# A graph attention layer on one core: the low parts of a dense group by two wide instructions, counts cleared on ScalarE, one register load per round of edge sums

## The chip, the cores and the metric

The kernel runs on one core of a Trainium2 chip. The metric is the device time of one execution in microseconds; the time before is the median of three runs. A core has five engines that work side by side, each through its own list of instructions in order: TensorE (PE, matrix products), VectorE (DVE, elementwise work and reductions), ScalarE (ACT), GpSimd (POOL, here gathers by indirect DMA) and SyncE (SP, here DMA issues). They wait for each other by semaphores. SBUF is the memory of 128 partitions that all engines work from, PSUM the accumulators that TensorE writes.

## The reference

The layer takes 12,500 nodes of 64 features and 400,000 edges of 64 features, the edges sorted by destination. Cut to what matters:

```python
h_src, h_dst = x[src], x[dst]
e = leaky_relu(concat([h_src, h_dst, efeats]) @ W_attn + b_attn)[:, 0]
m = concat([h_src, efeats]) @ W_ne
ex = exp(e - segment_max(e, dst)[dst])
alpha = ex / segment_sum(ex, dst)[dst]
z = segment_sum(alpha[:, None] * m, dst)
out = layernorm(x + relu(concat([x, z]) @ W_out))
```

Destinations are drawn as the square of a uniform number, so the first nodes have very many edges and the later ones few.

## The kernel before

**Groups and batches.** Edges go in groups of 512 (P = 128 partitions, T = 4 edges each): 782 groups. The first DG = 104 are the *dense* groups, whose 512 edges go to a few nodes at most (NODS: 2 to 6). The other 678 are *sparse* groups and go through the main loop in 44 batches of up to 16, each cut in *lots* of four groups. Per sparse lot, POOL gathers the source rows (L310), ScalarE and VectorE make the scores (L341 to L362), and TensorE multiplies the gathered rows by weighted one-hot columns (L763); VectorE adds the products into a ring of node sums (L780, in `add_in`).

**Dense groups without gathers.** A dense group doesn't gather. A source node's number is split in a *low* part (modulo 128) and a *high* part (0 to 97). The matrix `counts` [128, 98, 16] holds, for a low part (partition), a high part and one of 16 destination slots, the summed weights of the edges between them. `dense_counts(g)` makes it for one group as four matrix products, one for each of the T edges of a partition (L458): on the left `lows`, whose row for an edge has the edge's weight `kept` at its low part and zero elsewhere; on the right `highs`, a one-hot row over high part and slot that ScalarE makes (L450, L451). `lows` is made on VectorE by `tensor_scalar` (L453), one instruction for each t: compare `count_` (0 to 127, kept in PSUM) with the edge's low part, times its weight, 128x128. `dense_sum` adds the product to `counts` (L475, and L478 for a sixth node).

**Chunks.** 25 times, after 2 to 9 dense groups, a chunk is closed: `node_products` multiplies `counts` with all node rows, in 13 steps (L525); `node_pick` takes the wanted diagonal blocks out of the product on VectorE (L533, L536) and clears `counts` for the next chunk (L538, a memset of 128x1568, for all chunks but the last); `node_turn` (L544) and `node_sum` (L550) put the sums in place.

**Edge features.** The edge features of the dense groups are summed by `edge_products` (L510) and `edge_sum` (L518). `edge_sum` handles a round, the two or three groups of one batch rounded up to four or two adds: for each it loads the first node of the group from `dn` into a register (`node_of`) and adds at that place. There are 34 rounds of four adds and one of two.

**The order.** DVE, PE, ACT and SP run in the order in which the program is written (`manual_schedule`), POOL issues its gathers likewise. In each batch the lots' scores come first, and with them `node_products` and `edge_products` (first lot) and the counts of the batch's first dense group (second lot). Then comes the softmax, a chain in four phases over VectorE, ScalarE and TensorE (transposes L556 and L559, scans L664 to L699, `turned` at L563). Between its phases `dense_step(n)`, n = 0 to 3, is laid: at n = 0 `node_pick`, `edge_sum` and `dense_sum`, then products of the batch before (L763) and `node_turn`; at n = 1 `node_sum`; at n = 2 and n = 3 the counts of the second and third dense group; and at each n the source scores of the dense groups to come (`look_scores`, L436 to L442, with L411 on TensorE). The sum of the second group comes at n = 3; that of the third between the first weights of the batch's own lots (L749). So the order on VectorE at n = 3 is: L475 of the second group, L780, `lows` of the third group, the end of the softmax, L749 and L475 of the third.

**Buffers.** `lows` are tiles of 128x128 from a pool of LOWS = 6. `kept` and `low` are in SBUF.

Of the kernel before, what the change touches and what calls it, by code (L numbers as in the profile page):

```python
# [9 lines left out]
F32 = mybir.dt.float32  # L10
I32 = mybir.dt.int32
AF = mybir.ActivationFunctionType
OP = mybir.AluOpType
AX = mybir.AxisListType

P = 128
T = 4
# [8 lines left out]
S = 48  # L26
BG = 32
BIG = 6
LOWS = 6
SG = 4  # L30
BS = 16
DO = BS + 1
# [10 lines left out]
ND = 16  # L43
# [11 lines left out]
EngineType = mybir.EngineType  # L55


def sorted_path(ctx, tc, x, dst, idx, edge, w_ne, w_attn, b_attn, w_out, out, flag):
# [6 lines left out]
    nc = tc.nc  # L65
    N, D = x.shape
    E = edge.shape[0]
    NB = (N + P - 1) // P
# [6 lines left out]
    within = "a destination is a node"  # L75

    const = ctx.enter_context(tc.tile_pool(name="const", bufs=1))
# [32 lines left out]
    def nodes_of(g):  # L110
        return next(n for upto, n in NODS if g < upto)
# [4 lines left out]
    def round_of(g):  # L116
        return max(d for d in range(DB) if begins[d] <= g)

    def kept_at(g):
        d = round_of(g)  # L120
        return g - begins[d] + d % 2 * BD
# [3 lines left out]
    DN = DBL * P  # L125
# [47 lines left out]
    low, place = (const.tile([P, T, DG], F32, name=n) for n in ("low", "place"))  # L173
    high, slot_ = (const.tile([P, T, DG], BF16, name=n) for n in ("high", "slot_"))
    y_dense = const.tile([P, T, 2 * BD], F32, name="y_dense")
    kept = const.tile([P, T, 2 * BD], F32, name="kept")
# [4 lines left out]
    acce = const.tile([P, DN + NOD], F32, name="acce")  # L181
    nc.vector.memset(acce, 0.0)
    edge_both = const.tile([P, D], F32, name="edge_both")
    dn = const.tile([1, DG + 1], I32, name="dn")
    rel = const.tile([1, DG], I32, name="rel")
    counts = const.tile([P, NB, ND], F32, name="counts")
# [3 lines left out]
    nc.vector.tensor_reduce(node, ident.rearrange("p (h n) -> p n h", n=ND), axis=AX.X, op=OP.add)  # L190
    meet = const.tile([1, 2], I32, name="meet")
    of_next = const.tile([1, 4], F32, name="of_next")
    scrap_row = const.tile([1, 1], F32, name="scrap_row")

    loop = ExitStack()
# [5 lines left out]
    def cut(bank, *widths):  # L201
        at, out_ = 0, []
        for w in widths:
            out_.append(bank[:, at:at + w])
            at += w
        assert at <= 512
        return out_
# [19 lines left out]
    pens, sixth, count_ = cut(pps, 2 * P, P, P)  # L227
    sixth, w_dst = sixth[:, 0:NB], sixth[:, 0:D]
# [164 lines left out]
    def big():  # L393
        return work.tile([P, P, T], F32, name="big", bufs=BIG)
# [48 lines left out]

    def dense_counts(g):

        highs, lows = [], []
        wide = NB * min(FIT, nodes_of(g))
        for t in range(T):
            hi = big().rearrange("l p t -> l (p t)")[:, 0:wide]
            nc.scalar.activation(hi, places[:, 0:wide], AF.Square, bias=place[:, t, g:g + 1])  # L450
            nc.scalar.activation(hi, hi, AF.Relu, scale=-1.0, bias=1.0)  # L451
            lows.append(work.tile([P, P], F32, name="lows", bufs=LOWS))
            nc.vector.tensor_scalar(lows[t], count_, low[:, t, g:g + 1], kept[:, t, kept_at(g):kept_at(g) + 1],  # L453
                                    op0=OP.is_equal, op1=OP.mult)
            highs.append(hi)
        to = psum.tile([P, SG, P], F32, name="pg", bufs=4).rearrange("p a b -> p (a b)")[:, 0:wide]
        for t in range(T):
            nc.tensor.matmul(to, lows[t], highs[t], start=(t == 0), stop=(t == T - 1))  # L458
        if nodes_of(g) > FIT:
            hi = big().rearrange("l p t -> l (p t)")[:, 0:T * NB].rearrange("l (t h) -> l t h", t=T)  # L460
            for t in range(T):
                nc.scalar.activation(hi[:, t], places[:, wide:wide + NB], AF.Square, bias=place[:, t, g:g + 1])
            nc.scalar.activation(hi, hi, AF.Relu, scale=-1.0, bias=1.0)
            for t in range(T):
                nc.tensor.matmul(sixth, lows[t], hi[:, t], start=(t == 0), stop=(t == T - 1), skip_group_check=True)
        return g, to

    def dense_sum(g, to):
# [23 lines left out]
    def node_of(g):  # L492
        _, vs = nc.values_load_multi_w_load_instructions(
            dn[0:1, g:g + 1], engines=(EngineType.DVE,), min_val=0, max_val=DN - 1,
            skip_runtime_bounds_check_because=within)
        return vs[0]
# [15 lines left out]

    def edge_sum(g0, n, z):

        for c in range(n + n % 2):
            of = slice(c % 2 * D, (c % 2 + 1) * D)
            at = acce[of, ds(node_of(g0 + min(c, n - 1)), nodes_of(g0))]
            nc.vector.tensor_tensor(at, at, z[of, c, :], op=OP.add)  # L518

    def node_products(g0):  # L520
# [8 lines left out]
    def node_pick(g0, pairs):  # L529

        pr = feats.tile([P, SG, T, D], F32, name="pr", bufs=1)
        mine = pr[:, 0:2].rearrange("p g t f -> p (g t) f")
        nc.vector.tensor_tensor(mine, pairs.rearrange("p (h f) -> p h f", f=D),  # L533
                                own.unsqueeze(2).to_broadcast([P, HC, D]), op=OP.mult)
        sums_ = work.tile([P, D], F32, name="sums_", bufs=1)
        nc.vector.tensor_reduce(sums_, mine.rearrange("p h f -> p f h"), axis=AX.X, op=OP.add)  # L536
        if g0 + chunk_sizes[-1] < DG:
            nc.vector.memset(counts, 0.0)  # L538
        return g0, sums_

    def node_turn(g0, sums_, bank_):
# [277 lines left out]
    with before:  # L819
# [22 lines left out]
        with tc.manual_schedule(engines={EngineType.DVE, EngineType.Pool, EngineType.Activation, EngineType.PE, EngineType.SP}):  # L842
# [21 lines left out]
            for g0 in range(0, NG, 3 * P):  # L864
                n = min(3 * P, NG - g0)
# [5 lines left out]
            at = 0  # L871
# [32 lines left out]
    work = loop.enter_context(tc.tile_pool(name="work", bufs=2))  # L904
# [138 lines left out]
    with loop:  # L1043
# [55 lines left out]
        with tc.manual_schedule(engines={EngineType.PE, EngineType.DVE, EngineType.Activation, EngineType.SP}):  # L1099
# [11 lines left out]
            for k, G in enumerate(sizes):  # L1111
# [19 lines left out]
                for i, (g0, n) in enumerate(lots[k]):  # L1131
# [32 lines left out]
                    if k and i == 1 and batch_counts:  # L1164
                        open_counts.append(dense_counts(batch_counts[0]))
# [36 lines left out]
                def dense_step(n):  # L1202

                    nonlocal opened, summed, resolved_at, node_z
                    if n == 0 and opened:
                        opened = node_pick(*opened)
                    if n == 0 and summed:
                        edge_sum(*summed)
                        summed = None
# [23 lines left out]
                    if n > 1:  # L1233
                        for g in batch_counts[1:2] if n == 2 else batch_counts[2:]:
                            open_counts.append(dense_counts(g))

                fac, joint, carry, carry_d = drawn(softmax(k, about, carry, joined, dense_carry if joined is not None else None), dense_step)
                if fac_d is not None and k > fac_at[1]:
                    at = node_of(fac_at[0])
# [421 lines left out]
@with_exitstack  # L1661
def kernel(
    ctx: ExitStack,
    tc: tile.TileContext,
    x: bass.AP,
    dst: bass.AP,
    idx: bass.AP,
    edge: bass.AP,
    w_ne: bass.AP,
    w_attn: bass.AP,  # L1670
    b_attn: bass.AP,
    w_out: bass.AP,
    out: bass.AP,
):


    nc = tc.nc
    mark = ctx.enter_context(tc.tile_pool(name="mark", bufs=1))
    flag = mark.tile([1, 1], I32, name="flag")
    with ExitStack() as own:  # L1680
        sorted_path(own, tc, x, dst, idx, edge, w_ne, w_attn, b_attn, w_out, out, flag)
    odd = nc.values_load(flag[0:1, 0:1], min_val=0, max_val=1,
                         skip_runtime_bounds_check_because="it is zero or one")
    with tc.If(odd > 0):
        with ExitStack() as own:
            general_path(own, tc, x, dst, idx, edge, w_ne, w_attn, b_attn, w_out, out)
# [51 lines left out]
```

## Time and profile before

| | |
|---|---|
| time, median of 3 runs | 4354.64 us (4350.4 to 4369.21) |
| profiled execution: time / span | 4348.44 us / 4346.6 us |
| granted TensorE clock, mean | 0.666 |
| busy PE / DVE / ACT / POOL | 53% / 49% / 27% / 59% of the span |
| gathers on POOL (L310) | 2648, 2499.3 us |
| product of lows and highs (L458) | 832 records (two for one product), 493.3 us |
| lows (L453) | 416, 141.5 us |
| clears of counts (L538) | 24, 32.8 us |
| edge sums (L518) | 138 |

The times come from one profiled execution. Busy time counts instructions that compute; register loads are not in it. In the rows of groups the columns are: line, engine, operation, tile written and tiles read, shape, count, busy time in us and mean of one in ns, and the idle time of the engine just before these instructions with what ended most of it. In the time line: start in us, duration, engine, line, operation, and in brackets how long the engine had been idle before and what it waited for ("issue": nothing that the profile shows). Records of matmuls show when TensorE takes them up; their results come later when older work is still in the array.

### The profile page before, as it was taken

The numbers are of one execution on the slowest core, as the hardware profiler recorded it, in microseconds if no ns is written. First come the engines' busy times: TensorE is split into PE (matmuls) and PEld (weight loads), VectorE is DVE, ScalarE is ACT, GpSimd is POOL, SyncE is SP. The second block draws the span as 40 slices with busy tenths as digits, with TensorE's granted clock in tenths as the row PEclk, the third lists the DMA queues.
The fourth block names the chain that finished last, engine by engine and source line by source line (L and its number), as shares of the span: only waits on it lengthen the run. The fifth ranks groups of instructions, "written<-read, shape, count | busy, mean of one in ns | idle before, by whom it ended". The sixth has DMA issues, their size and how long they took to land. (4 is left out here: it accounts for less than half of the span.)

```text
span 4346.6 us, 35943 instructions
## 1 busy us (share of the span) xinstructions
PE 2307.0 (53%) x9391; PEld 1840.8 (42%) x9391; DVE 2116.4 (49%) x5395; ACT 1165.9 (27%) x2586; POOL 2568.5 (59%) x2728
## 2 busy tenths in 40 slices
PE   0143344554555554655566665666566655565843
PEld 0143344444444444444444443444444434443543
DVE  4343344444444454554445554555555444453645
ACT  0111122222222232222223232332333223333312
POOL 6666666666556666566555655566555645555462
PEclk9999996555555555666566666666666656565655
DMA  9232223223232232322222222222223212222221
GB/s 116 57 64 52 53 55 73 56 56 69 45 67 57 55 63 58 68 54 57 56 58 63 60 55 56 56 57 58 56 57 74 57 31 47 50 49 43 58 46 26
DMA packets 497933, 248.42 MB, mean 57 GB/s; under 512 B 332351, under 2 KB 454286, under 8 KB 497718
## 3 DMA queue, kind: packets, MB, share of 16 engines
q1 hardware_dynamic: 407506, 155.16, 15.2%
q0 software_dynamic: 87008, 90.47, 13.6%
q8 instruction: 78, 1.28, 0.1%
q10 hardware_dynamic: 3204, 0.39, 0.1%
q14 instruction: 137, 1.12, 0.1%
HBM read 239.02 MB, written 6.77 MB: 57 GB/s over the span
## 5 line engine op out<-in xcount | busy, mean ns | idle before, releaser
L310 POOL DMA_INDIRECT zx<-table,srcs x2648 | 2499.3, 944 | 1683.0 <-issue 1239.6
L763 PE MATMUL pg<-w,zx 128*128 128x16 f32 (+9 forms) x5280 | 1042.6, 359 | 602.6 <-issue 548.0
L763 PEld LDWEIGHTS pg<-w,zx 128*128 128x128 f32 x5280 | 1061.4, 302 | 608.1 <-issue 549.0
L458 PE MATMUL pg<-big,lows 128*128 128x490 f32 (+3 forms) x832 | 493.3, 747 | 486.1 <-DVE lows L453 204.2
L458 PEld LDWEIGHTS pg<-big,lows 128*128 128x128 f32 x832 | 237.5, 300 | 669.7 <-issue 473.5
L525 PE MATMUL pg<-xall,counts 128*128 128x512 f32 (+1 forms) x650 | 326.7, 664 | 4.4 <-DVE var L1024 2.4
L344 DVE TENSOR_TENSOR pr<-ze,fixed 128x1024 f32<-128x1024 f32 (+3 forms) x176 | 207.5, 1179 | 224.4 <-issue 95.5
L411 PE MATMUL pg<-s_src,big 128*128 128x98 f32 x832 | 228.2, 433 | 164.1 <-issue 145.0
L556 PE MATMUL lines<-ident,bnd 128*1 128x128 f32 x176 | 52.8, 391 | 462.7 <-issue 342.1
L450 ACT ACTIVATE big<-places,place 128x490 f32<-128x490 int16 (+3 forms) x416 | 249.5, 600 | 155.3 <-remote 153.2
L411 PEld LDWEIGHTS pg<-s_src,big 128*128 128x128 f32 x832 | 209.0, 327 | 171.2 <-issue 170.6
L475 DVE TENSOR_TENSOR counts<-counts,pg 128x490 f32 (+3 forms) x104 | 58.1, 558 | 391.4 <-remote 311.4
L780 DVE TENSOR_TENSOR acc<-acc,pg 128x32 f32 (+9 forms) x678 | 125.8, 186 | 234.2 <-PE pg L763 106.0
L438 DVE TENSOR_TENSOR pr<-pr,pg 128x392 f32<-128x392 f32 x104 | 58.5, 562 | 354.9 <-remote 175.3
L346 DVE TENSOR_REDUCE fixed<-pr 128x16 f32<-128x1024 f32 (+3 forms) x176 | 209.2, 1188 | 32.2 <-issue 14.0
L451 ACT ACTIVATE big<-big 128x490 f32<-128x490 f32 (+3 forms) x416 | 217.2, 522 | 13.2
L556 PEld LDWEIGHTS lines<-ident,bnd 128*1 128x1 f32 x176 | 14.6, 98 | 485.9 <-issue 360.1
L525 PEld LDWEIGHTS pg<-xall,counts 128*128 128x128 f32 (+1 forms) x650 | 137.6, 219 | 188.8 <-issue 188.8
L563 ACT ACTIVATE line<-tops 1x256 f32<-1x256 f32 x44 | 29.0, 659 | 624.7 <-DVE tops L665 381.6
L342 ACT ACTIVATE zx<-ze 128x1024 f32<-128x1024 f32 (+3 forms) x176 | 181.0, 1028 | 8.3 <-issue 1.3
L341 ACT ACTIVATE fixed<-wrow 128x144 f32<-128x144 f32 (+9 forms) x176 | 46.0, 262 | 506.7 <-issue 321.7
L453 DVE TENSOR_SCALAR lows<-pps,low,kept 128x128 f32<-128x128 f32 x416 | 141.5, 403 | 0.0
(335 smaller groups left out, 2474.2 us busy)
## 6 DMA issues: line engine op xcount, KB each, us to landing
ze<-in_edge_dram SPq DMA_DIRECT2D x160, 512.0 KB
zx<-table,srcs POOLq DMA_INDIRECT x2648
low_of<-low_rows SPq DMA_DIRECT2D x104, 128.0 KB
ep<-in_edge_dram SPq DMA_DIRECT2D x104, 128.0 KB
ed<-in_edge_dram SPq DMA_DIRECT2D x34, 384.0 KB
table<-xall SPq DMA_DIRECT2D x7, 455.0 KB
ze<-in_edge_dram SPq DMA_DIRECT2D x8, 384.0 KB
out_dram<-yo SPq DMA_DIRECT2D x23, 128.0 KB
```

Of the source, the lines that this page charges most:

```text
L310: nc.gpsimd.indirect_dma_start(out=zx[0:r, g, t, 1:EW] if plain else zx[0:r, g, t, 0:EW], out_offset=None, in_=x[:, :] if plain else table ...
L342: nc.scalar.activation(zx[0:r, 0:n, :, EW:EW + D], ze[0:r, 0:n], AF.Copy)
L344: nc.vector.tensor_tensor(pr[0:r, 0:n], ze[0:r, 0:n], w_edge[0:r].unsqueeze(1).to_broadcast([r, n, T, D]), op=OP.mult)
L346: nc.vector.tensor_reduce(ysum[0:r, 0:n], pr[0:r, 0:n], axis=AX.X, op=OP.add)
L411: nc.tensor.matmul(found[:, t, :], hot[:, :, t], s_src, start=True, stop=True)
L450: nc.scalar.activation(hi, places[:, 0:wide], AF.Square, bias=place[:, t, g:g + 1])
L451: nc.scalar.activation(hi, hi, AF.Relu, scale=-1.0, bias=1.0)
L453: nc.vector.tensor_scalar(lows[t], count_, low[:, t, g:g + 1], kept[:, t, kept_at(g):kept_at(g) + 1], op0=OP.is_equal, op1=OP.mult)
L458: nc.tensor.matmul(to, lows[t], highs[t], start=(t == 0), stop=(t == T - 1))
L525: nc.tensor.matmul(pairs[0:m * ND, 0:m * D], counts[:, h0:h0 + m, :].rearrange("l h n -> l (h n)"), xall[:, h0:h0 + m, 1:EW], start=(h0 == ...
L763: nc.tensor.matmul(pg[:, g, :], zx[:, g, t, 1:EW + D], w[:, g, t, :], start=(t == 0), stop=(t == T - 1))
L780: nc.vector.tensor_tensor(ag, ag, pg[:, g, :], op=OP.add)
```

## The change

Three edits. First, `lows` of a group becomes one tile [128, 4, 128], made by two VectorE instructions of 128x512: a comparison of `count_` with the low parts, both broadcast, and then a product in place with the weights, broadcast; the tile comes from a pool of three. Their place in VectorE's order is where the four were. Second, `counts` is cleared by a ScalarE copy of a broadcast column of zeros instead of a VectorE memset; on ScalarE it stands between `bnd` of the softmax's first phase and L563. Third, `edge_sum` loads the registers of a round by one load instead of one for each add. The orders of PE, POOL and SP are the same as before.

```diff
-LOWS = 6
+LOWS = 3
...
+    zero_col = const.tile([P, 1], F32, name="zero_col")
+    nc.vector.memset(zero_col, 0.0)
...
     def dense_counts(g):

-        highs, lows = [], []
+        highs = []
+        lows = work.tile([P, T, P], F32, name="lows", bufs=LOWS)
+        nc.vector.tensor_tensor(lows, count_.unsqueeze(1).to_broadcast([P, T, P]),
+                                low[:, :, g:g + 1].to_broadcast([P, T, P]), op=OP.is_equal)
+        nc.vector.tensor_tensor(lows, lows, kept[:, :, kept_at(g):kept_at(g) + 1].to_broadcast([P, T, P]), op=OP.mult)
         wide = NB * min(FIT, nodes_of(g))
         for t in range(T):
             hi = big().rearrange("l p t -> l (p t)")[:, 0:wide]
             nc.scalar.activation(hi, places[:, 0:wide], AF.Square, bias=place[:, t, g:g + 1])
             nc.scalar.activation(hi, hi, AF.Relu, scale=-1.0, bias=1.0)
-            lows.append(work.tile([P, P], F32, name="lows", bufs=LOWS))
-            nc.vector.tensor_scalar(lows[t], count_, low[:, t, g:g + 1], kept[:, t, kept_at(g):kept_at(g) + 1],
-                                    op0=OP.is_equal, op1=OP.mult)
             highs.append(hi)
...
-            nc.tensor.matmul(to, lows[t], highs[t], start=(t == 0), stop=(t == T - 1))
+            nc.tensor.matmul(to, lows[:, t], highs[t], start=(t == 0), stop=(t == T - 1))
...
     def edge_sum(g0, n, z):

+        _, vs = nc.values_load_multi_w_load_instructions(
+            dn[0:1, g0:g0 + n], engines=(EngineType.DVE,), min_val=0, max_val=DN - 1,
+            skip_runtime_bounds_check_because=within)
         for c in range(n + n % 2):
             of = slice(c % 2 * D, (c % 2 + 1) * D)
-            at = acce[of, ds(node_of(g0 + min(c, n - 1)), nodes_of(g0))]
+            at = acce[of, ds(vs[min(c, n - 1)], nodes_of(g0))]
             nc.vector.tensor_tensor(at, at, z[of, c, :], op=OP.add)
...
         if g0 + chunk_sizes[-1] < DG:
-            nc.vector.memset(counts, 0.0)
+            nc.scalar.activation(counts.rearrange("p h n -> p (h n)"), zero_col.to_broadcast([P, NB * ND]), AF.Copy)
```

More of the change, by code (lines that the diff above doesn't have):

```diff
@@ L464, in dense_counts @@
             for t in range(T):
-                nc.tensor.matmul(sixth, lows[t], hi[:, t], start=(t == 0), stop=(t == T - 1), skip_group_check=True)
+                nc.tensor.matmul(sixth, lows[:, t], hi[:, t], start=(t == 0), stop=(t == T - 1), skip_group_check=True)
         return g, to
```

## The prediction

> **What bounds the kernel now.** I read the page first (busy times, then the costliest groups), then the list of waits, then the time line of single batches in the dense stage, which is where all three edits lie.
>
> ```profile
> PE 2307.0 (53%) x9391; PEld 1840.8 (42%) x9391; DVE 2116.4 (49%) x5395; ACT 1165.9 (27%) x2586; POOL 2568.5 (59%) x2728
> L310 POOL DMA_INDIRECT zx<-table,srcs x2648 | 2499.3, 944 | 1683.0 <-issue 1239.6
> L458 PE MATMUL pg<-big,lows 128*128 128x490 f32 (+3 forms) x832 | 493.3, 747 | 486.1 <-DVE lows L453 204.2
> L453 DVE TENSOR_SCALAR lows<-pps,low,kept 128x128 f32<-128x128 f32 x416 | 141.5, 403 | 0.0
> ```
>
> No engine is full. The gathers on POOL are the nearest to it: 0.944 us each and, as the time line shows, 0.30 us of issue after each, so 1.24 us is their shortest period and 400 us could hold 322 of them. A table of POOL by stretches of 400 us shows about 260 in the dense stage, so POOL has a fifth of its time free there:
>
> ```profile
> 1400.00:1800.00 400.00, 244.50 (x260) 0.59 0.29 59
> 2200.00:2600.00 400.00, 235.28 (x250) 0.64 0.28 59
> 2287.90 0.94 POOL L310 DMA_INDIRECT zx<-table,srcs  x1 [0.30 <-issue]
> ```
>
> What does set the pace is that PE and DVE, both in an order written by hand, wait for each other. In the list of waits (total, times, longest) DVE waits for PE's sums and PE for DVE's lows; "remote" is a semaphore whose sender the profile doesn't name, and on these lines only PE's product can be it:
>
> ```profile
> DVE counts L475 <- remote: 311.4, 30, 21.8
> PE pg L458 <- DVE lows L453: 204.2, 27, 32.3
> DVE pr L438 <- PE pg L411: 74.3, 25, 10.3
> ```
>
> A time saved or lost on DVE counts only where PE is idle and waits for DVE; where DVE waits for PE afterwards it is swallowed. So each edit has to be placed.
>
> **Lows.** Four 128x128 comparisons-with-product of 0.403 us, overlapping to 1.36 us in all, become two 128x512 instructions on VectorE, at the same place in its order. Rows by shape give their price: a comparison of a PSUM operand with a broadcast one over 512, and a product over 512.
>
> ```profile
> L353 DVE TENSOR_TENSOR hot<-fixed,drel 128x512 bf16<-128x512 f32 x20 | 13.8, 692 | 4.2 <-DVE fixed L351 3.6
> L358 DVE TENSOR_TENSOR pr<-hot,fixed 128x512 f32<-128x512 bf16 x20 | 13.7, 687 | 2.7 <-DVE hot L353 2.1
> L488 DVE TENSOR_TENSOR wd<-wd,kept 128x20 f32<-128x20 f32 x27 | 5.0, 185 | 1.5 <-DVE wd L486 0.6
> L486 DVE TENSOR_TENSOR wd<-fixed,slot__119 128x20 f32<-128x20 f32 x27 | 4.6, 169 | 1.3 <-ACT keep L725 0.9 <-issue 0.4
> ```
>
> 0.69 + 0.69 and some 0.04 between dependent instructions is 1.42 us: DVE's own time changes by +0.06 us per group, 104 x 0.06 = 6 us, nothing much. But PE's first matmul of a group needs only the first of the four tiles, ready 0.40 us after the start; now it needs both instructions, so it can begin 1.42 - 0.40 = 1.02 us later. In 65 of the 104 groups it is gated so, beginning 0.52 to 0.6 us after the lows do; here the first of them, a batch in the middle, another, and the last:
>
> ```profile
> 576.87 1.36 DVE L453 TENSOR_SCALAR lows<-pps,low,kept 128x128 f32<-128x128 f32 x4
> 577.42 2.95 PE L458 MATMUL pg<-big,lows 128*128 128x196 f32 x8 [0.41 <-DVE acc L780]
> ...
> 2812.30 1.36 DVE L453 TENSOR_SCALAR lows<-pps,low,kept 128x128 f32<-128x128 f32 x4
> 2812.85 5.93 PE L458 MATMUL pg<-big,lows 128*128 128x490 f32 x8 [2.84 <-DVE acc L780]
> 2822.17 0.67 DVE L475 TENSOR_TENSOR counts<-counts,pg 128x490 f32 x1 [8.09 <-remote]
> 2823.52 1.36 DVE L453 TENSOR_SCALAR lows<-pps,low,kept 128x128 f32<-128x128 f32 x4
> 2824.07 5.45 PE L458 MATMUL pg<-big,lows 128*128 128x490 f32 x8 [5.08 <-ACT big L450]
> 2829.55 0.67 DVE L475 TENSOR_TENSOR counts<-counts,pg 128x490 f32 x1 [0.19 <-PE pg L458]
> 2831.53 2.54 PE L763 MATMUL pg<-w,zx 128*128 128x36 f32 x22
> ...
> 3019.23 0.87 DVE L780 TENSOR_TENSOR acc<-acc,pg 128x36 f32 x4 [0.39 <-issue]
> 3020.01 1.36 DVE L453 TENSOR_SCALAR lows<-pps,low,kept 128x128 f32<-128x128 f32 x4
> 3020.57 6.18 PE L458 MATMUL pg<-big,lows 128*128 128x490 f32 x8 [8.29 <-DVE lows L453]
> 3026.78 0.67 DVE L475 TENSOR_TENSOR counts<-counts,pg 128x490 f32 x1 [3.88 <-PE pg L458]
> ...
> 4019.52 1.36 DVE L453 TENSOR_SCALAR lows<-pps,low,kept 128x128 f32<-128x128 f32 x4
> 4020.07 6.48 PE L458 MATMUL pg<-big,lows 128*128 128x490 f32 x8 [32.28 <-DVE lows L453]
> ```
>
> All 34 third groups of a batch (the one of 2823.52) are gated, 28 of the second groups (2812.30), and only 3 of the first ones, which find PE behind with older work.
>
> Third groups: PE has been idle for 5 us, the counts of the second group are out, and what follows on PE (L763 of the next lots) comes straight behind. So the delay passes on. By the time line 20 of the 34 have their next L763 with no idle time before it; in the other 14 PE waits there a little, mostly for weights that VectorE makes, and I let half the delay pass: 20 x 1.02 + 14 x 0.5 = 27 us.
>
> Second groups: the sum at L475 comes 9.3 us after the matmuls' start at 2812.85 but 6.2 us after it at 3020.57, though the matmuls are of one size. Where PE had waited 2.84 us by the records it was still working off older matmuls, and a later start costs nothing; where it had waited 8.29 us it was empty and the delay passes on. The sum follows the last matmul within 0.1 us in 7 groups, like that of 3026.78. 7 x 1.02, and a tenth of it in the other 21, make 9 us.
>
> Lows together: +36 us; the bounds are 0 (PE always behind) and 65 x 1.02 = 66 us.
>
> The product has two SBUF operands, while large operands of this kernel mostly sit in PSUM. L488 against L486 is the nearest pair: two SBUF operands took 0.185 us, one of them in PSUM 0.169 us, with gathers running for three quarters of the time. If the product were blocked behind a gather (0.944 us), that small one would show 0.3 us and more. So I take 0.69, and keep as the upper end 0.69 plus half a gather at three quarters, 0.35 us.
>
> **Counts on ScalarE.** 24 clears of 1.365 us leave VectorE; two chunk batches, the first figures being start and duration:
>
> ```profile
> L538 DVE MEMSET counts<- 128x1568 f32 x24 | 32.8, 1365 | 6.6 <-issue 6.6
> 2273.16 1.36 DVE L538 MEMSET counts<- 128x1568 f32 x1 [0.28 <-issue]
> 2277.62 0.15 DVE L518 TENSOR_TENSOR acce<-acce,pg 64x4 f32 x1 [3.09 <-PE pg L763]
> 2278.17 0.16 DVE L518 TENSOR_TENSOR acce<-acce,pg 64x4 f32 x1 [0.40 <-issue]
> 2283.12 0.65 ACT L563 ACTIVATE line<-tops 1x256 f32<-1x256 f32 x1 [28.30 <-DVE tops L670]
> ...
> 2581.65 1.36 DVE L538 MEMSET counts<- 128x1568 f32 x1 [0.28 <-issue]
> 2582.93 0.48 DVE L518 TENSOR_TENSOR acce<-acce,pg 64x4 f32 x3
> 2592.18 0.56 DVE L438 TENSOR_TENSOR pr<-pr,pg 128x392 f32<-128x392 f32 x1 [4.13 <-PE pg L411]
> ```
>
> In about 8 of the 24 (2273) the next add waits for PE anyway, here 3.09 us: worth nothing. In the other 16 (2581) VectorE runs on, but the next L438 waits for PE, here 4.13 us. PE at that time goes through its products, not through anything that VectorE does later there. I let a quarter through: 4 x 1.365 = 5.5 us. Bounds 0 and 16 x 1.64 = 26 us.
>
> The clear on ScalarE: by rows of that engine, 0.630 us for 512 and 1.060 us for 1024, so 1.52 us for 1568.
>
> ```profile
> L401 ACT ACTIVATE big<-big 128x512 f32<-128x512 f32 x104 | 65.5, 630 | 3.3
> L342 ACT ACTIVATE zx<-ze 128x1024 f32<-128x1024 f32 x160 | 169.6, 1060 | 7.7 <-issue 1.3 <-DMA zx<-table,srcs 0.4
> ```
>
> It waits for the chunk's matmuls, which were done when the memset began at 2273.16; queued behind it on ScalarE stands L563 of 2283.12, which waited 28.30 us for VectorE. The next add into the counts stands on VectorE behind the adds of 2277.62 and after, over 4 us later. So the clear is hidden; without that cover it is 24 x 1.5 = 36 us.
>
> **One load per round.** 34 full rounds had four loads, about 0.40 us ahead of its add (2278.17); the row at 3019.23 shows what one load ahead of four adds looks like, 0.39 us once. So 3 x 0.40 = 1.2 us go in the 15 rounds or so where the loads stood in the open (2277.62); in most of the later ones (2582.93) they had been fetched during the clear. With the clear gone, those come into the open: one load now, not four. Of 15 x 1.2 = 18 us a quarter passes, since the same L438 or L475 waits for PE next: 4.5 us. Bounds 0 and 34 x 1.2 = 41 us.
>
> **Sum.** +36 - 5.5 - 4.5 = +26 us on the profiled execution's 4348.4 (its span is 4346.6): 4374. The median of the runs lies 6.2 us above that execution, so 4380.
>
> **Rivals.**
> *All is swallowed.* PE is behind with older work after the third groups too, as the 9.3 us at 2812.85 suggest, and the gains drown in L438's waits: 4340 to 4365.
> *Faster.* The lows' delay is swallowed, and VectorE is more often last than I read, so that half to all of the gains count. The bounds of 26 and 41 us are not both to be had whole, as the loads that now come into the open cost some of it: 20 to 50 us less than the 4354.6 of the median, 4305 to 4335. It decides as soon as L438 and L475 after a chunk stop waiting for PE. Against it: 74.3 and 311.4 us of such waits.
> *Slower, in full.* PE is empty at the second groups too, since what looked like old work is only its own latency: 66 us. If the product and the gathers also block each other, 65 x 0.35 = 23 us more: 4415 to 4440. It decides once the product shows well over 0.7 us. For: the pacing by PE. Against: L488.
> The Trainium skill's page "SBUF — State Buffer", section "Who interferes with whom", says that a VectorE instruction with two SBUF inputs contends with a GpSimd instruction that reads SBUF, and that the one that starts later blocks for the whole of the other. By it this rival would hold in its dearer form; L488, the one small case in this trace, shows no sign of it, and no large case stands there.
> *It doesn't do what it says:* the built kernel has 208 such instructions, 24 clears on ScalarE and one load a round; below 1%.
>
> **How the numbers follow.** A difference of 0.5%, 22 us, is about what a measurement of this kernel can tell from none. Chances: forecast 0.40 (4360 to 4400, of which 0.25 lies above 4376 and 0.15 below), swallowed 0.17, faster 0.18, in full 0.25. Faster 0.18, same 0.15 + 0.17 = 0.32, slower 0.25 + 0.25 = 0.50. The range from 4315 to 4430 leaves out the lower part of the faster case and the upper part of the full one, some 0.07 each; the forecast's own range is 4360 to 4400.
>
> **What would show it.** Right: two DVE instructions of 0.69 us per group, matmuls beginning some 1.5 us after the lows' start, the idle time before third groups' L458 longer by 1 us, L563 unchanged behind a clear of 1.5 us, rounds of four adds within 0.7 us, more waiting at L438. Wrong: a product well over 0.8 us or gathers over 1 us (then they block each other); L475's waits unchanged and the batches as long as before (swallowed); batches shorter in the chunk phases by over 1 us (faster).

## The result and the profile after

| | before | after |
|---|---|---|
| median of 20 runs each, us | 4356.37 (4336.67 to 4381.26) | 4374.98 (4361.15 to 4382.71) |
| ratio, with its 95% interval | | 1.0033 [1.0019, 1.0048] |
| profiled execution: span, us | 4346.6 | 4378.3 |

The change makes the kernel slower by a third of a per cent: 14 us by the ratio, 19 us by the medians. The forecast was 4380 us. The measured 4374.98 lies in the forecast's own range (4360 to 4400), with the sign as foretold and in the part of that range below 0.5%.

Two rows of the changed kernel's page, then four of its groups, then three of its waits, to be read against those shown of before:

```profile
PE 2284.7 (52%) x9391; PEld 1825.9 (42%) x9391; DVE 2087.1 (48%) x5164; ACT 1202.9 (27%) x2610; POOL 2575.5 (59%) x2728
L312 POOL DMA_INDIRECT zx<-table,srcs x2648 | 2505.8, 946 | 1710.9 <-issue 1238.5
```

```profile
L461 PE MATMUL pg<-big,lows 128*128 128x490 f32 (+3 forms) x832 | 482.3, 739 | 536.5 <-DVE lows L452 334.7
L452 DVE TENSOR_TENSOR lows<-lows,kept 128x512 f32<-128x512 f32 x104 | 72.3, 695 | 3.6
L450 DVE TENSOR_TENSOR lows<-pps,low 128x512 f32<-128x512 f32 x104 | 71.1, 684 | 0.0
L544 ACT ACTIVATE counts<-zero_col 128x1568 f32<-128x1568 f32 x24 | 36.2, 1507 | 187.2 <-remote 153.5 <-PE lines L562 20.6 <-PE pg L461 12.2
```

```profile
PE pg L461 <- DVE lows L452: 334.7, 46, 35.4
DVE counts L478 <- remote: 296.2, 26, 26.6
DVE pr L440 <- PE pg L413: 90.5, 25, 7.8
```

Every price of an instruction came out: 0.684 and 0.695 us for the two wide instructions, 1.507 us for the clear on ScalarE. DVE is busy 29 us less in all, and the span is 32 us longer. What grew is TensorE's wait for the lows, 334.7 us instead of 204.2, and, by 6.5 us, the time of the gathers on POOL, which the change doesn't touch. Not all of the first is new: TensorE's whole idle time before these matmuls grew by 50 us, from 486.1 to 536.5, so the rest had stood there before under other names.

The time line of a batch like the one of 2812 before:

```profile
2831.24 0.68 DVE L450 TENSOR_TENSOR lows<-pps,low 128x512 f32<-128x512 f32 x1
2831.96 0.69 DVE L452 TENSOR_TENSOR lows<-lows,kept 128x512 f32<-128x512 f32 x1
2832.80 4.98 PE L461 MATMUL pg<-big,lows 128*128 128x490 f32 x8 [5.41 <-DVE lows L452]
```

TensorE begins 1.56 us after the lows' start, where it was 0.55: 1.01 us later. And a chunk batch, the one that was shown at 2581 before:

```profile
2589.79 1.51 ACT L544 ACTIVATE counts<-zero_col 128x1568 f32<-128x1568 f32 x1 [6.27 <-remote]
2589.79 0.69 DVE L539 TENSOR_TENSOR pr<-pg,own 128x512 f32<-128x512 f32 x1 [6.72 <-remote]
2591.48 0.70 DVE L524 TENSOR_TENSOR acce<-acce,pg 64x4 f32 x4
2595.26 0.67 DVE L478 TENSOR_TENSOR counts<-counts,pg 128x490 f32 x1 [1.11 <-PE pg L461]
2601.23 0.56 DVE L440 TENSOR_TENSOR pr<-pr,pg 128x392 f32<-128x392 f32 x1 [4.13 <-PE pg L413]
```

The clear starts with L539 on the same release and is hidden, and the four adds of a round take 0.70 us together. The next L440 waits 4.13 us for TensorE, exactly as before.

### The profile page after: what moved, and what is told of

Read it like the earlier page. It is cut to its first block, busy times and chain, and to the rows that moved or that the text cites. A ratio compares the mean times of both kernels' runs of the same rounds, so it can differ in the third digit from the quotient of the medians.

```text
span 4378.3 us, 35319 instructions
## 1 busy us (share of the span) xinstructions
PE 2284.7 (52%) x9391; PEld 1825.9 (42%) x9391; DVE 2087.1 (48%) x5164; ACT 1202.9 (27%) x2610; POOL 2575.5 (59%) x2728
## 3 DMA queue, kind: packets, MB, share of 16 engines
q0 software_dynamic: 87008, 90.47, 11.2%
## 5 line engine op out<-in xcount | busy, mean ns | idle before, releaser
L769 PE MATMUL pg<-w,zx 128*128 128x16 f32 (+9 forms) x5280 | 1032.2, 356 | 593.3 <-issue 544.1
L769 PEld LDWEIGHTS pg<-w,zx 128*128 128x128 f32 x5280 | 1050.1, 299 | 599.7 <-issue 543.3
L461 PE MATMUL pg<-big,lows 128*128 128x490 f32 (+3 forms) x832 | 482.3, 739 | 536.5 <-DVE lows L452 334.7
L440 DVE TENSOR_TENSOR pr<-pr,pg 128x392 f32<-128x392 f32 x104 | 58.5, 562 | 371.8 <-remote 187.3
L355 DVE TENSOR_TENSOR hot<-fixed,drel 128x576 bf16<-128x576 f32 (+9 forms) x176 | 110.7, 629 | 29.1 <-DVE fixed L353 14.7
```

The lines of the kernel that those rows point to most:

```text
L355: nc.vector.tensor_tensor(hot[0:r, 0:n], slots[0:r, 0:Sk].unsqueeze(1).unsqueeze(1).to_broadcast([r, n, T, Sk]), drel[0:r, :, b:b + n].rea ...
L461: nc.tensor.matmul(to, lows[:, t], highs[t], start=(t == 0), stop=(t == T - 1))
L769: nc.tensor.matmul(pg[:, g, :], zx[:, g, t, 1:EW + D], w[:, g, t, :], start=(t == 0), stop=(t == T - 1))
```

## The experiments

All are compared with the kernel before on the same chip. **The chips differ.** In the measurement above the kernel before takes 4356 us. Of the four chips of the experiments one is like that (4318 us); on three the same kernel takes 3461 to 3468 us. The chip of the measurement above is called the first chip here, those three the quicker ones. First POOL's row in the list of waits, of the kernel before on the first chip, then the same row of the kernel with only the register loads changed on one of the quicker ones, and last the gathers of the latter in two stretches of 400 us (busy us and count, granted clock, DMA share, GB/s):

```profile
POOL zx L310 <- issue: 1261.5, 2596, 33.9
```

```profile
POOL zx L310 <- issue: 754.3, 2475, 0.3
```

```profile
400.00:800.00 400.00, 302.37 (x321) 0.82 0.31 69
3000.00:3400.00 400.00, 302.48 (x321) 0.65 0.28 62
```

With 0.944 us and 0.30 us of issue, 322 gathers are what 400 us can hold: on the quicker chips POOL never stops and the gathers set the pace. On the first chip POOL stands still at times, up to 33.9 us. I take it from the waits that TensorE and VectorE set the pace in the dense stage there; no run tests this by itself. There the time line of the kernel before has stretches like this one, in which TensorE takes up an instruction only every 1.4 us with no releaser shown:

```profile
2842.59 0.22 PE L763 MATMUL pg<-w,zx 128*128 128x36 f32 x1 [1.90 <-issue]
2843.99 0.22 PE L763 MATMUL pg<-w,zx 128*128 128x36 f32 x1 [1.19 <-issue]
```

In all, TensorE is idle for 602.6 us before the matmuls of this line in that trace, and for 13.1 us in that of the kernel with only the register loads changed on a quicker chip. Why the chips differ was not settled, and neither was how much of the time on the first chip these stretches take. It makes two cases of every experiment: in one a step counts if it delays a gather, in the other also if it delays TensorE.

### One edit at a time (a quicker chip, before 3467.93 us)

The diffs are the parts of the change's diff: for the first kernel `LOWS` and `dense_counts`, for the second `zero_col` and the clear in `node_pick`, for the third `edge_sum`.

> The wide lows alone; clears and register loads as before. Theory 1 (PE's first matmul of a group starts about 1.0 us later, and about half of that passes on): +20 to +40 us against before, ratio 1.005 to 1.009, a little more than the whole change's +14 us, as the other two edits pay some back. Rival (the lows cost nothing; the clear on ScalarE or the register loads make the kernel slower): within 5 us of before.

3477.17 us, ratio 1.0028 [1.0017, 1.0039]: slower by 9.7 us by the ratio, 9.2 by the medians.

> Only the clear of counts moves to ScalarE. Theory 1 (in most chunk batches VectorE waits for PE's products at L438 or L518 next, which swallows the 1.36 us saved): -12 to 0 us. Rival A (VectorE is last after a chunk): -20 to -33 us. Rival B (the clear delays something on ScalarE): +5 us or more.

3467.54 us, ratio 1.0000 [0.9991, 1.0009].

> Only the rounds of edge sums change: one register load for up to four adds. Theory 1 (three loads of 0.40 us less in some 15 of 34 rounds, mostly swallowed by the next wait for PE): -10 to 0 us. Rival (VectorE is last there): -18 to -41 us.

3467.43 us, ratio 0.9999 [0.9990, 1.0008]. So on this chip the whole cost is in the lows, and the other two edits move nothing.

### Is it the late first tile?

```diff
-            lows.append(work.tile([P, P], F32, name="lows", bufs=LOWS))
-            nc.vector.tensor_scalar(lows[t], count_, ...
+            t_ = t
+            t = T - 1 - t_
+            lows.insert(0, work.tile([P, P], F32, name="lows", bufs=LOWS))
+            nc.vector.tensor_scalar(lows[0], count_, ...
```

> The kernel before with the four lows of a group made in the order t = 3, 2, 1, 0, while PE still takes t = 0 first: the same instructions and the same VectorE time, one SBUF operand fewer than in the wide form, but the first matmul has to wait for the last of the four, 0.95 us later. Theory 1 (the cost is the later first tile): as slow as the wide lows alone, +15 to +35 us. Rival (the cost is the wide form itself: two SBUF operands beside the gathers): within 5 us of before.

3466.66 us, ratio 0.9998 [0.9989, 1.0007]: no cost. The delay was there, as the waits of TensorE show, of this kernel first and of the one with only the register loads changed second:

```profile
PE pg L460 <- DVE lows L455: 105.5, 70, 2.9
```

```profile
PE pg L458 <- DVE lows L453: 52.0, 32, 1.9
```

TensorE waited twice as long, and no more gathers were long: 14 lasted over 0.96 us here, 11 in the run with only the loads changed. (Their sum is 6 us longer in this profile, 2505.7 us against 2499.6, because most gathers took some 3 ns more, the median being 0.947 us instead of 0.944. The same is so in the profile of the kernel with the clear and the loads changed, 2506.3 us on the third quicker chip, which has the lows of before. The cause of these 3 ns is open.) On a chip where the gathers set the pace, my theory falls: the 9.7 us are not the late first tile. What did differ with the wide lows were single long gathers. The time line of the whole change on the next chip, around one product:

```profile
1350.28 0.94 POOL L312 DMA_INDIRECT zx<-table,srcs  x1 [0.30 <-issue]
1351.53 0.95 POOL L312 DMA_INDIRECT zx<-table,srcs  x1 [0.30 <-issue]
1351.87 0.68 DVE L450 TENSOR_TENSOR lows<-pps,low 128x512 f32<-128x512 f32 x1
1352.59 0.69 DVE L452 TENSOR_TENSOR lows<-lows,kept 128x512 f32<-128x512 f32 x1
1352.78 1.32 POOL L312 DMA_INDIRECT zx<-table,srcs  x1 [0.30 <-issue]
1354.40 0.95 POOL L312 DMA_INDIRECT zx<-table,srcs  x1 [0.30 <-issue]
```

The gather of 1351.53 is under way when the comparison starts (one operand in PSUM) and isn't touched. That of 1352.78 starts while the product with two SBUF operands runs, takes 1.32 us instead of 0.94, and ends 0.82 us after the product's end. So it is with the gathers that start during a product, from some 0.05 us after its start to 0.14 us before its end: there were 38 in this trace, all of them ended 0.81 or 0.82 us after the product, and together they took 10.2 us more than 0.944 us each. One that had started before the product, or at most 0.05 us after it, ran its 0.94 us as ever; the product then took 0.69 us too, or up to 0.77 in the few cases where both started at once.

### Late first tile and two SBUF operands, taken apart (another quicker chip, before 3461.37 us)

> The whole change, on the chip of this comparison. If the chip is like that of the first experiments, where the gathers on POOL set the pace and both kernels take about 3468 us: +8 to +12 us, as the wide lows alone gave +9.7 and the other two edits nothing. If it is like that of the first measurement (4356 us): +14 us again.

3471.86 us, ratio 1.0031 [1.0020, 1.0042].

```diff
-    kept = const.tile([P, T, 2 * BD], F32, name="kept")
...
-    ends, ini, pp, w_src = cut(lines, 2 * P, 8, T * BS, D)
+    ends, ini, pp, w_src, kept = cut(lines, 2 * P, 8, T * BS, D, T * 2 * BD)
+    kept = kept.rearrange("p (t g) -> p t g", t=T)
```

> The wide lows alone, but with the weights kept in PSUM instead of SBUF, so that the product has one SBUF operand; all else, the late first tile too, as in the wide lows alone. Theory 2 (the product with two SBUF operands holds up gathers: in the wide-lows runs some 25 to 35 gathers lasted 1.02 to 1.46 us instead of 0.944, all but a few of them beside a product): no long gathers beside products, and within 3 us of before where gathers set the pace. Theory 1 (late first tile): as slow as the wide lows alone, +10 us or more.

3460.44 us, ratio 0.9999 [0.9990, 1.0008].

```diff
                 def dense_step(n):
...
+                    if n > 1:
+                        for g in batch_counts[1:2] if n == 2 else batch_counts[2:]:
+                            lows_of[g] = dense_lows(g)
                     if seen:
                         look_scores(*seen.pop(0))
```

`dense_lows` makes the lows as `dense_counts` did, and that takes them from `lows_of`. The lows of before, made early in the second of the next two runs, have a pool of 8 tiles there instead of 6.

> The wide lows alone, made earlier on VectorE for the second and third group of a batch (ahead of the source scores and of the counts' sum in their phases), so that TensorE doesn't wait for them; the product with two SBUF operands stays. Theory 2: +6 to +12 us where gathers set the pace, with the long gathers still there. Theory 1: before's time or less; where TensorE and VectorE set the pace (4356 us), 20 to 60 us less than before.

3472.48 us, ratio 1.0033 [1.0020, 1.0045].

> The kernel before with its own four-instruction lows made earlier in the same way: neither a late first tile nor two SBUF operands in a large product. Theory 2: within 3 us of before where gathers set the pace. Theory 1: as before there, and 20 to 60 us less than before where TensorE and VectorE set the pace.

3461.44 us, ratio 0.9999 [0.9990, 1.0008].

| | first tile late | first tile early |
|---|---|---|
| product with two SBUF operands | +10.5 us (whole change) | +11.1 us |
| one of them in PSUM, or lows of before | -0.9 us | +0.1 us |

Only the rows matter, not the columns. The groups of gathers, in the order wide with the weights in PSUM, whole change, early wide, early lows of before:

```profile
L310 POOL DMA_INDIRECT zx<-table,srcs x2648 | 2500.2, 944 | 807.1 <-issue 744.3 <-DMA zx<-table,srcs 30.5 <-PE pg L764 4.6
```

```profile
L312 POOL DMA_INDIRECT zx<-table,srcs x2648 | 2510.3, 948 | 807.1 <-issue 744.9 <-DMA zx<-table,srcs 26.8 <-PE pg L769 5.8
```

```profile
L310 POOL DMA_INDIRECT zx<-table,srcs x2648 | 2509.9, 948 | 807.0 <-issue 741.5 <-DMA zx<-table,srcs 27.1 <-PE pg L771 4.3
```

```profile
L310 POOL DMA_INDIRECT zx<-table,srcs x2648 | 2499.5, 944 | 807.1 <-issue 744.0 <-DMA zx<-table,srcs 29.9 <-PE pg L771 3.4
```

POOL's idle time is the same to 0.1 us in all four; its busy time is 10 us longer in the two whose product has two SBUF operands, and that is their whole loss. (In all four the median gather took 0.944 us.) By single gathers, 47 and 49 of theirs lasted over 0.96 us, with 13.1 and 12.2 us above 0.944 in sum; in the other two it was 15 and 14, with 2.9 and 2.5 us.

### A larger dose, on a chip like the first (before 4317.71 us)

Both build on the wide lows with the weights in PSUM.

```diff
+        nc.vector.tensor_tensor(lows, lows, lows, op=OP.mult)
         nc.vector.tensor_tensor(lows, lows, kept..., op=OP.mult)
```

> The wide lows with the weights in PSUM (which cost nothing), and between comparison and product one more 128x512 product: lows with itself, zeros and ones, so the values stay as they are. It is again an instruction of 0.69 us with two SBUF operands, one for each of the 104 groups. Theory 2 (a gather that starts while such a product runs is held until the product ends): some 45 to 55 gathers beside it longer than 0.96 us, 12 to 13 us of POOL time, and +10 to +13 us where gathers set the pace. If it is VectorE's time or the late first tile: the same as in the run with the comparison made twice.

4350.01 us, ratio 1.0071 [1.0052, 1.0089].

```diff
         nc.vector.tensor_tensor(lows, count_..., low..., op=OP.is_equal)
+        nc.vector.tensor_tensor(lows, count_..., low..., op=OP.is_equal)
         nc.vector.tensor_tensor(lows, lows, kept..., op=OP.mult)
```

> The same kernel with the comparison made twice instead: also 0.69 us more on VectorE and as much later a first matmul for each group, but one operand is in PSUM. Theory 2: within 4 us of before where gathers set the pace, and no longer gathers. Theory 1 or VectorE's time: as slow as the run with the extra product. Where TensorE and VectorE set the pace (4356 us): +10 to +60 us by theory 1, as the first matmul comes 1.7 us later than before.

4339.35 us, ratio 1.0050 [1.0034, 1.0065]. Two rows of its time line show one group:

```profile
2194.00 0.68 DVE L448 TENSOR_TENSOR lows<-pps,low 128x512 f32<-128x512 f32 x1
2196.35 4.57 PE L461 MATMUL pg<-big,lows 128*128 128x392 f32 x8 [9.34 <-DVE lows L452]
```

The first matmul comes 2.35 us after the lows' start, as it does in the median of the groups that wait so, which is 1.8 us later than the 0.55 of before. Without any held gather that costs 21.6 us here: the delay does count on this kind of chip. What VectorE spends on the third instruction is in these 21.6 us, and the run doesn't part the two. The product in place of the second comparison has 45 gathers over 0.96 us against 13, 11.2 us in sum against 2.6, and costs 10.7 us more; the two intervals overlap, so that difference, unlike those on the quicker chips, is not clear of noise. The busy time of POOL doesn't show it either, since in the run with the comparison the median gather took 0.947 us instead of 0.944.

### What is left over (a third quicker chip, before 3468.23 us)

> The wide lows with the weights in PSUM once more: the late first tile alone, without held gathers. Where gathers set the pace (3460 us): within 3 us of before, as it was. Where TensorE and VectorE set the pace (4320 to 4360 us): by theory 1, +8 to +20 us, in proportion to the +21.6 us that a first matmul 1.7 us later cost there; if only the gathers mattered there too, 0.

3468.28 us, ratio 1.0000 [0.9991, 1.0009].

> The clear on ScalarE and the single register load together, with the lows of before. Where gathers set the pace: within 3 us of before, as each alone. Where TensorE and VectorE set the pace: -20 to 0 us by the prediction's sum (-10); -20 to -50 us if VectorE is last after a chunk.

3468.93 us, ratio 1.0002 [0.9993, 1.0011]. Both were meant for a chip like the first and met a quicker one, where they repeat what was known: a late first tile costs nothing there, and neither edit pays. So the late first tile alone, the other two edits, and the lows made early were never measured on a chip like the first. Nothing tried beats the kernel before.

## Why the prediction was right, and where it was not

**The sign and the size** came out, but in part by luck. The forecast was 25 us over the time before, and 14 to 19 were measured. By the estimates below its largest term, the late first tile, was about three times too large, and the hold-up of the gathers, which the sum put at nothing and left to a rival, made up for a part of that.

**The late first tile.** All its observable steps are as written: the matmuls begin 1.56 - 0.55 = 1.01 us later (1.02 foretold), all third groups are gated, and TensorE is idle longer ahead of them. The term itself, +36 us, was too large, as far as is known. 1.8 us of delay cost 21.6 us on the chip like the first; in proportion (an estimate, and rather a high one, as the third instruction's time on VectorE is in it) 1.01 us costs 12. The step that failed, then, is the share that passes on, three quarters in the third groups. It was read from TensorE's queue alone; where the rest of the delay is made up further on was not traced. On the quicker chips the share is zero, as the late tile alone shows there (-0.9 and 0.05 us).

**Two SBUF operands.** I took 0.69 us and no contention, because L488 with two SBUF operands took hardly longer than L486. That row could not show it: I looked for a longer VectorE instruction and the loss is on POOL. By what the large product shows, a gather is held if it starts between 0.05 us after the instruction's start and 0.14 us before its end, and of 0.185 us that leaves nothing. (The gathers were also busy for 0.59 of the time around L488, not for three quarters of it, which is reached only with the 0.30 us of issue counted in.) The rival's price of 23 us, 0.35 us for each of 65 products, was too high; the measured one is 104 products for 10 us where gathers set the pace. My sign for it, "gathers over 1 us", was the right one: 25 gathers of the changed kernel on the first chip lasted over 1 us against 8 before, and 31 against 13 over 0.96 us, with 8.8 us in sum against 2.2. What the Trainium skill's page "SBUF — State Buffer" says in "Who interferes with whom", that the instruction that starts later blocks, agrees with the gathers here on one side: a gather that starts later waits for the product's end. On the other side the trace differs: a product that starts during a gather isn't held for the rest of it. In the changed kernel on the first chip 81 of the 104 products did so, and took 0.693 us in the mean, against 0.695 of all.

**The clear and the loads.** The clear is hidden on ScalarE as foretold, and each edit alone is within 1 us on a quicker chip, where the gathers set the pace. For the first chip the -10 us were not measured alone. Two rows of the time line of before stand beside the chunk batch shown above:

```profile
2579.63 0.69 DVE L533 TENSOR_TENSOR pr<-pg,own 128x512 f32<-128x512 f32 x1 [5.31 <-remote]
2586.21 0.67 DVE L475 TENSOR_TENSOR counts<-counts,pg 128x490 f32 x1 [0.46 <-PE pg L458]
```

From the one to the other it was 6.58 us, and in the changed kernel, from 2589.79 to 2595.26, it is 5.47. The 1.1 us between them are not the memset's, since VectorE waits for TensorE's product at this sum in both kernels, and that product was quicker in the changed one:

```profile
2579.82 6.35 PE L458 MATMUL pg<-big,lows 128*128 128x490 f32 x8
2589.98 5.17 PE L461 MATMUL pg<-big,lows 128*128 128x490 f32 x8
```

The granted clock was 0.55 in the first of these stretches and 0.67 in the second. What the two edits shortened is VectorE's way to that wait, 6.12 us before and 4.36 after. Over all 24 such batches the sum came sooner after L533 by 0.1 to 1.8 us, 1.1 in the mean, in the 15 where the adds follow without a wait in both kernels; in two others it came 2.5 and 4.5 us later, behind a longer wait ahead of the adds. Whether more or less than my quarter is kept in the end is not shown, since the next L438 or L440 waits for TensorE again. With 12 us for the tile and 7 to 10 us for the gathers (6.5 us of POOL's time in the changed kernel, 10.7 us between the two runs of the larger dose), 19 to 22 us together, the measured 14 to 19 us leave 0 to -8 us for both edits. That is worked out, not shown, and it assumes that what the gathers lose passes on whole on a chip where they don't set the pace.

**The bound.** "No engine is full" and POOL with a fifth of its time free was right for the trace I had and holds on one chip of the experiments. On three others POOL is the bound throughout. The free time that I counted on didn't exist on those.

## What to carry to other kernels

Before a VectorE instruction with a PSUM operand or a scalar is replaced by one with two large SBUF operands, look whether POOL issues gathers at that time, and put one operand in PSUM: here that took the whole cost away where gathers set the pace. To find such a loss look at the durations of the other engine's instructions, not of the one that is suspected, since a small instruction next to a long wait shows nothing. A wide instruction in place of four small ones also delays the first consumer by the difference to the first small one; here that cost nothing where another engine, POOL, set the pace.

## What was not expected of the hardware

- A gather on POOL that starts while VectorE multiplies two SBUF operands (128x512, 0.69 us), up to 0.14 us before the end, is held and ends 0.82 us after that instruction, so that it takes 1.46 us at most instead of 0.944. One that started a little earlier is not, and a comparison of the same size with one PSUM operand holds none.
- The same kernel takes 4318 to 4356 us on two chips and 3461 to 3468 us on three, and only the traces of the slower ones have many stretches of 1.4 us per instruction on TensorE: its idle time before the matmuls of the gathered rows is 516 to 603 us there and 6 to 21 us on the quicker ones.
